# Expert tiles in four pieces, the last four tiles behind a branch

## The chip, the cores and the metric

The kernel runs on one core of one Trainium2 chip. The metric is the device time of one execution in microseconds (us). Engines are named as in the profile: PE (matmuls), PEld (its weight loads), DVE, ACT, POOL, and SP, which issues most DMAs.

## What is computed

A network of four blocks over 4096 tokens of 256 features: differential attention, a two-layer local attention with feed-forward, a diffusion block and a mixture of experts. Only the last one is touched. For each token a gate chooses two of eight experts; each expert is a two-layer network with a layer norm between:

```python
gates = jax.nn.softmax(xf @ gate_w, axis=-1)
topw, topi = jax.lax.top_k(gates, K)                 # K = 2 of E = 8
topw = topw / jnp.sum(topw, axis=-1, keepdims=True)
combine = jnp.sum(topw[:, :, None] * jax.nn.one_hot(topi, E, dtype=xf.dtype), axis=1)
h = jnp.einsum('td,edh->teh', xf, w1) + b1           # 256 -> 512
h = _ln(h, ln1_g, ln1_b)
h = jax.nn.gelu(h, approximate=False)
y = jnp.einsum('teh,ehd->ted', h, w2) + b2           # 512 -> 256
out = jnp.einsum('ted,te->td', y, combine)
out = _ln(out + xf, ln_g, ln_b)
```

## The kernel before

Routing. As each of eight sequences of 512 tokens leaves the diffusion block, `gate` ranks the experts and scatters each token's row twice into a DRAM table `xrows`, sorted by expert, with the token's number in an extra column. Each expert has room for all 4096 tokens. After the last sequence `table` (L1320) counts the rows of each expert, rounds up to tiles of 128 rows (`ntiles`), and sums them up (`end`); its last entry is the number of tiles that hold rows. From that it makes `table_`: for each of `TILES` = 2 x 4096 / 128 + 8 = 72 tiles the row where it starts and the offsets of its expert's weights. 72 is the most that any routing can need. Tiles past the last one with rows read rows that were filled in advance and write to rows that nobody reads.

Tiles. `experts` (L1355) walks over all 72 tiles, with all experts' weights in SBUF. `value` reads one entry of the table into a register of one engine. For tile n:

- `load` (L1377): SP loads 128 rows (`ex`, six buffers), up to four tiles ahead.
- `hidden` (L1383): DVE makes `eto`, the rows to which the results go (six buffers); PE transposes the rows (`ext`), ACT copies them (`exT`); PE multiplies by w1 (`ph`, two PSUM buffers); DVE adds the bias (`eh`), takes the statistics (`st`, `mv`); POOL makes the reciprocal deviation (`rs`, L172 and L173); DVE normalizes `eh` in place (L194).
- `outer` (L1400): PE transposes `eh` (`eht`), ACT takes the Gelu with the norm's scale and bias in four instructions (`ehT`), PE multiplies by w2 (`py`), DVE adds the bias (`ey`), POOL scatters the 128 rows to the DRAM table `yrows` at `eto` (L1413). `ext` and `eht` share three PSUM buffers.

The loop at L1466 does `hidden(n)` and then `outer(n - 3)`, so three tiles are on their way at once. `between()` puts small work between tiles: the diagonal matrices of combine weights `edw` for four sequences.

The order of instructions on each engine is made when the program is built, by a scheduler: it takes the program order as priority and moves a later instruction ahead where an earlier one is not ready by its model of the times. Within one engine the order is then fixed, and each instruction waits for those that it needs.

Finish. When all scatters have landed, `finish` (L1417) takes for each sequence the normalized input (`xfb`) and the two results of each token (`egot`) from DRAM, adds them with their weights on PE (`pz`), norms twice and adds the residual. Two of the `xfb` loads do not depend on the tiles.

One branch is there already: at L955 every engine loads a flag into a register, and L956 chooses between two variants of the diffusion block. The given inputs take the first, so that after it the code of the other is jumped over.

Of the kernel before, what the change touches and what calls it, by code (L numbers as in the profile page):

```python
# [16 lines left out]
P = 128  # L17
# [16 lines left out]
NE = 8  # L34
EH = 2 * D
EC = EH // P
CAP = NB * S
TILES = 2 * CAP // P + NE
ROWS = NE * CAP + NE * P
HOLD = 1000  # L40

# [79 lines left out]
class Net:  # L121
# [77 lines left out]
    def turned(self, ps, src, dst, scale=None, bias=None):  # L199

        nc = self.nc
        for c in range(src.shape[2] // P):
            pt = ps.tile([P, S], F32, name="pt", tag="ps")
            for t in range(NT):
                nc.tensor.transpose(pt[:, t * P:(t + 1) * P], src[:, t, c * P:(c + 1) * P], self.ident)
            if scale is None:
                self.copy(dst[:, c, :], pt)
            else:
                nc.scalar.activation(dst[:, c, :], pt, AF.Identity, bias=bias[:, c:c + 1], scale=scale[:, c:c + 1])
# [1014 lines left out]
    def load_routes(self, ctx):  # L1224

        w = ctx.enter_context(self.tc.tile_pool(name="routes", bufs=1))
        self.gatew = w.tile([P, DC, NE], F32, name="gate", tag="gate")
        self.nc.sync.dma_start(self.gatew, self.a["L1_ffn_gate_w"].rearrange("(c p) f -> p c f", p=P))
        self.routes = w
        self.slots = [w.tile([P, 2 * NT], mybir.dt.int32, name=f"slots{b}", tag=f"slots{b}") for b in range(NB)]  # L1230
        self.vals = [w.tile([P, 2, 2, NT], F32, name=f"val{b}", tag=f"val{b}") for b in range(NB)]
        self.runs = [w.tile([P, NT + 1, NE], F32, name=f"run{b}", tag=f"run{b}") for b in range(NB)]
        self.table_ = w.tile([P, 4, TILES], mybir.dt.int32, name="table", tag="table")

    def row_of(self, c, n):
        return self.const[:, c:c + n]
# [83 lines left out]
    def table(self, run, wk, small, ps):  # L1320

        nc, row = self.nc, self.row_of
        tie = row(C_TIE, NE * NE).rearrange("p (e f) -> p e f", f=NE)
        cap, tiles = CAP, TILES
        pc = ps.tile([P, NE], F32, name="pcount", tag="ps")
        self.mm(pc, [(row(C_ONE, P), run[:, NT, :])])
        n = small.tile([P, NE], F32, name="count", tag="count", bufs=1)
        nc.vector.tensor_copy(n, pc)
        thr = row(C_STEP, cap // P)
        over = small.tile([P, NE, cap // P], F32, name="over", tag="eover", bufs=1)  # L1330
        nc.vector.tensor_tensor(over, n.unsqueeze(2).to_broadcast([P, NE, cap // P]),
                                thr.unsqueeze(1).to_broadcast([P, NE, cap // P]), ALU.is_gt)
        nt = small.tile([P, NE], F32, name="ntiles", tag="ntiles", bufs=1)
        nc.vector.tensor_reduce(nt, over, AX.X, ALU.add)
        m = small.tile([P, NE, NE], F32, name="upto", tag="upto", bufs=1)
        nc.vector.tensor_mul(m, tie, nt.unsqueeze(1).to_broadcast([P, NE, NE]))
        end = small.tile([P, NE], F32, name="end", tag="end", bufs=1)
        nc.vector.tensor_reduce(end, m, AX.X, ALU.add)
        nc.vector.tensor_add(end, end, nt)
        ge = wk.tile([P, 2, tiles, NE], F32, name="past", tag="th")  # L1340
        tile_i = row(C_TILE, tiles)
        nc.vector.tensor_tensor(ge[:, 0], tile_i.unsqueeze(2).to_broadcast([P, tiles, NE]),
                                end.unsqueeze(1).to_broadcast([P, tiles, NE]), ALU.is_ge)
        nc.vector.tensor_mul(ge[:, 1], ge[:, 0], nt.unsqueeze(1).to_broadcast([P, tiles, NE]))
        es = small.tile([P, 2, tiles], F32, name="estart", tag="estart", bufs=1)
        nc.vector.tensor_reduce(es, ge, AX.X, ALU.add)
        f = small.tile([P, 4, tiles], F32, name="offsets", tag="offsets", bufs=1)
        nc.vector.tensor_sub(f[:, 0], tile_i, es[:, 1])
        nc.vector.tensor_scalar(es[:, 1], es[:, 0], float(cap), None, ALU.mult)
        nc.vector.scalar_tensor_tensor(f[:, 0], f[:, 0], float(P), es[:, 1], ALU.mult, ALU.add)  # L1350
        for i, by in enumerate((DC * EH, EH + D, 2 * EC)):
            nc.vector.tensor_scalar(f[:, 1 + i], es[:, 0], float(NE - 1), float(by), ALU.min, ALU.mult)
        nc.vector.tensor_copy(self.table_, f)

    def experts(self, nb, rest):  # L1355

# [4 lines left out]
        with ExitStack() as ctx:  # L1361
# [4 lines left out]
            nc, tc, g = self.nc, self.tc, self.ew  # L1366
# [6 lines left out]
            def value(i, k, engine, top):  # L1373
                return nc.values_load(self.table_[0:1, k, i:i + 1], engines=[engine], min_val=0, max_val=top,
                                      skip_runtime_bounds_check_because="the table's expert and row are bounded as they are made")

            def load(i):  # L1377
                x = wk.tile([P, D + 1], F32, name="ex", tag="ex", bufs=6)
                r = value(i, 0, mybir.EngineType.SP, ROWS - P)
                nc.sync.dma_start(x, self.rows[bass.ds(r, P), :])  # L1380
                return x

            def hidden(i, x):  # L1383
                to = small.tile([P, 1], mybir.dt.int32, name="eto", tag="eto", bufs=6)
                nc.vector.tensor_tensor(to, x[:, D:D + 1], self.const[:, C_DUMP + i:C_DUMP + i + 1], ALU.min)
                pt = pst.tile([P, DC, P], F32, name="ext", tag="pst")
                for c in range(DC):
                    nc.tensor.transpose(pt[:, c, :], x[:, self.tok(c)], self.ident)
                xT = wk.tile([P, DC, P], F32, name="exT", tag="exT")
                nc.scalar.copy(xT, pt)  # L1390
                e = value(i, 1, mybir.EngineType.PE, (NE - 1) * DC * EH)
                eb = value(i, 2, mybir.EngineType.DVE, (NE - 1) * (EH + D))
                ph = psh.tile([P, EH], F32, name="ph", tag="psh")
                self.mm(ph, [(xT[:, c, :], w1[:, bass.ds(e + c * EH, EH)]) for c in range(DC)])
                h = wk.tile([P, EH], F32, name="eh", tag="eh", bufs=4)
                nc.vector.tensor_add(h, ph, bias[:, bass.ds(eb, EH)])
                self.norm(small, [h], [h])
                return h, e, eb, to

            def outer(i, h, e, eb, to):  # L1400
                pt = pst.tile([P, EC, P], F32, name="eht", tag="pst")
                for c in range(EC):
                    nc.tensor.transpose(pt[:, c, :], h[:, self.tok(c)], self.ident)  # L1403
                en = value(i, 3, mybir.EngineType.Activation, (NE - 1) * 2 * EC)
                hT = wk.tile([P, EC, P], F32, name="ehT", tag="ehT")
                for c in range(EC):
                    nc.scalar.activation(hT[:, c, :], pt[:, c, :], AF.Gelu, bias=scales[:, bass.ds(en + EC + c, 1)],  # L1407
                                         scale=scales[:, bass.ds(en + c, 1)])
                py = psy.tile([P, D], F32, name="py", tag="psy")
                self.mm(py, [(hT[:, c, :], w2[:, bass.ds(e + c * D, D)]) for c in range(EC)])  # L1410
                y = wk.tile([P, D], F32, name="ey", tag="ey", bufs=4)
                nc.vector.tensor_add(y, py, bias[:, bass.ds(eb + EH, D)])
                i = nc.gpsimd.indirect_dma_start(self.got[:, :], bass.IndirectOffsetOnAxis(ap=to, axis=0), y, None)  # L1413
                tc.declare_no_dep(i.ins, group="store", reason="results have rows of their own")
                tc.add_to_no_dep_group("store", i.ins)
# [46 lines left out]
            between = Between()  # L1462
            for b in range(min(4, nb)):
                between.add(weights(b))
            loaded, made = {}, {}
            for n in range(TILES + 3):  # L1466
                for j in range(n, min(n + 4, TILES)):
                    if j not in loaded:
                        loaded[j] = load(j)
                if n < TILES:  # L1470
                    made[n] = hidden(n, loaded.pop(n))
                if n >= 3:
                    outer(n - 3, *made.pop(n - 3))
                between()
            between.end()
            tiles.close()
            psf = ctx.enter_context(tc.tile_pool(name="e_psf", bufs=6, space=PSUM))
            self.joint()
# [79 lines left out]
```

## Time and profile before

| what | us |
|---|---|
| median of three timed runs (lowest, highest) | 3854.63 (3848.53, 3860.05) |
| the profiled execution's own time | 3837.43 |
| its span, first to last instruction | 3835.7 |
| first and last expert transpose `ext` start | 3374.9, 3719.7 |
| first and last scatter of results start | 3401.88, 3740.41 |
| first `egot` load issued | 3742.8 |

The granted clock of PE was 0.953 on average over the span. The profile has, for each instruction, its start and length, and for each idle time of an engine what ended it. A line number can be that of a helper: `mm` (L213) issues most matmuls, so they are told apart by the tile's name. Lengths of matmuls overlap, since PE is pipelined.

### The profile page before, as it was taken

To read this page: it belongs to the slowest core of one execution; us is meant where nothing else is said; L and a number is where in the kernel's file an instruction comes from. 1 tells how busy PE (TensorE), PEld (TensorE's weight loads), DVE (VectorE), ACT (ScalarE), POOL (GpSimd) and SP (SyncE) were. 2 spreads that over 40 slices of the span, in tenths; PEclk is the share of its full clock that TensorE was granted. 3 is DMA by queue.
4 is the path that set the end of the run, shared out by engine and by line. 5 is a ranking of instruction groups with operands and counts; after the bars stand their busy time and mean duration, and the time that the engine had idled before them with its cause. 6 is when DMAs were issued, how large, how long until landed. Compare 5 with 4: busy or idle time off the path is not lost. (4 is left out here: it accounts for less than half of the span.)

```text
span 3835.7 us, 53567 instructions
## 1 busy us (share of the span) xinstructions
PE 3484.9 (91%) x20034; PEld 1894.1 (49%) x20034; DVE 2201.1 (57%) x4364; ACT 1855.1 (48%) x3719; POOL 1583.6 (41%) x1432
## 2 busy tenths in 40 slices
PE   8999999999987999999999999997988889679985
PEld 3344444444434566665665555564444444446554
DVE  6777777677646666665555666663244443344445
ACT  3555555555543444444444444443655555223334
POOL 3666766676654433333333343321012211153334
PEclk8999999999979999999999999998999999789997
DMA  9300000000001000000010000000000000421115
GB/s 350 119 1 7 6 7 1 7 7 1 6 6 34 3 4 4 4 4 25 4 34 9 9 9 9 9 20 23 1 23 23 23 17 17 147 68 55 53 43 167
DMA packets 95138, 130.29 MB, mean 34 GB/s; under 512 B 24702, under 2 KB 73242, under 8 KB 94874
## 3 DMA queue, kind: packets, MB, share of 16 engines
q1 hardware_dynamic: 88346, 108.94, 8.8%
q0 software_dynamic: 6528, 17.87, 1.3%
q8 instruction: 162, 2.65, 0.3%
q14 instruction: 102, 0.84, 0.1%
HBM read 57.40 MB, written 65.18 MB: 32 GB/s over the span
## 5 line engine op out<-in xcount | busy, mean ns | idle before, releaser
L372 ACT ACTIVATE e<-sa 128x1024 f32<-128x1024 f32 (+3 forms) x512 | 359.4, 702 | 303.7 <-PE sa L365 299.3
L393 POOL TENSOR_TENSOR e<-e,e 128x1536 f32<-128x1536 f32 (+2 forms) x192 | 451.7, 2353 | 91.4 <-PE po L388 81.4
L365 PE MATMUL sa<-qT,kT 32*128 32x512 f32 (+3 forms) x2048 | 431.9, 498 | 9.2 <-ACT e L372 8.8
L369 DVE TENSOR_REDUCE spread<-sc 128x2 f32<-128x256 f32 (+3 forms) x512 | 422.2, 825 | 15.3
L355 PE MATMUL sc<-kT,qT 32*128 32x128 f32 (+3 forms) x2048 | 421.6, 493 | 7.9 <-DVE spread L369 4.5
L656 ACT ACTIVATE lp<-lp,lnm 128x256 f32<-128x256 f32 (+1 forms) x512 | 240.1, 470 | 260.4 <-DVE lnm L648 156.0
L660 POOL TENSOR_TENSOR lp<-lp,lrs 128x1024 f32<-128x1024 f32 x64 | 121.1, 1893 | 529.0 <-DVE lrs L657 508.9
L368 DVE TENSOR_TENSOR sc<-sc,const 128x256 f32<-128x256 f32 x512 | 218.6, 427 | 173.7 <-PE sa L365 140.7
L1088 ACT ACTIVATE te<-tsa 128x1024 f32<-128x1024 f32 x256 | 248.9, 1023 | 135.8 <-PE tsa L1084 88.7
L355 PEld LDWEIGHTS sc<-kT,qT 32*128 32x128 f32 x2048 | 160.7, 189 | 284.9 <-DVE spread L369 113.1
L213 PE MATMUL lpa<-ghT,lw 128*128 128x512 f32 x640 | 284.8, 600 | 12.1 <-ACT ghT L569 12.1
L213 PE MATMUL lqk<-qkv,lhT 128*128 128x512 f32 x512 | 247.7, 622 | 2.3 <-DVE qk L607 1.6
L608 POOL TENSOR_TENSOR qk<-qk,over 128x1024 f32<-128x1024 f32 x64 | 151.4, 2366 | 207.8 <-DVE qk L607 207.8
L375 POOL TENSOR_SCALAR_AFFINE_SELECT e<-e 128x512 f32<-128x512 f32 x256 | 160.5, 640 | 177.0 <-ACT e L372 176.6
L1407 ACT ACTIVATE ehT<-eht,enorm 128x128 f32<-128x128 f32 x288 | 108.3, 457 | 208.6 <-PE eht L1403 207.7
L213 PEld LDWEIGHTS lpa<-ghT,lw 128*128 128x128 f32 x640 | 119.3, 190 | 163.3 <-issue 136.3
L388 PE MATMUL po<-e,v 128*32 128x512 f32 (+3 forms) x2048 | 188.3, 451 | 4.0 <-POOL e L375 3.6
L365 PEld LDWEIGHTS sa<-qT,kT 32*128 32x128 f32 x2048 | 160.9, 190 | 56.4 <-ACT e L372 29.7
L645 DVE TENSOR_TENSOR lp<-lsc,const 128x768 f32<-128x768 f32 (+1 forms) x128 | 138.6, 1083 | 86.5 <-PE lsc L642 85.9
L642 PE MATMUL lsc<-lkT,lqT 64*128 64x256 f32 (+1 forms) x1024 | 156.9, 386 | 28.1 <-DVE qk L607 28.0
L1084 PE MATMUL tsa<-tqT,tkT 32*128 32x512 f32 x1024 | 170.2, 673 | 5.9 <-DVE tqT L1039 3.3
L213 PE MATMUL py<-ew,ehT 128*128 x576 | 145.3, 397 | 23.5 <-ACT ehT L1407 23.5
(294 smaller groups left out, 6811.7 us busy)
## 6 DMA issues: line engine op xcount, KB each, us to landing
xrows<-zero SPq DMA_DIRECT2D x66, 514.0 KB
ex<-xrows SPq DMA_DIRECT2D x72, 128.5 KB
ew<-in_L_ffn_w_dram SPq DMA_DIRECT2D x16, 512.0 KB
egot<-yrows SPq DMA_DIRECT2D x16, 512.0 KB
x<-in_L_attn_X_dram SPq DMA_DIRECT2D x8, 512.0 KB
saved<-x SPq DMA_DIRECT2D x8, 512.0 KB
lx<-saved SPq DMA_DIRECT2D x8, 512.0 KB
xf<-xf SPq DMA_DIRECT2D x8, 512.0 KB
```

What stands on the lines that cost most here:

```text
L213: self.nc.tensor.matmul(out, lhsT=l, rhs=r, start=i == 0, stop=i == len(pairs) - 1)
L355: nc.tensor.matmul(sc[:, i, :w], lhsT=qT[g, self.tok(t)], rhs=kT[g, :w], start=True, stop=True)
L365: nc.tensor.matmul(sa[:, i, :S - k * P], lhsT=kT[g, self.tok(k)], rhs=qT[g, k * P:], start=True, stop=True)
L368: nc.vector.tensor_add(sc[:, :, w - P:w], sc[:, :, w - P:w], own)
L369: nc.vector.tensor_reduce(self.spread[n % 2][:, t, g0:g0 + 2, 0 if n % 2 else 16], sc[:, :, :w], AX.X, ALU.max, negate=True)
L372: nc.scalar.activation(x[:, h0:h0 + 2, :], sa[:, :, :S - k * P], AF.Exp, scale=0.25)
L375: nc.gpsimd.affine_select(x[:, :, :P], x[:, :, :P], [[0, 4], [1, P]], ALU.is_ge, 0.0, base=0, channel_multiplier=-1)
L388: nc.tensor.matmul(pos[n][group(g), k * P:], lhsT=seqs[b][1][:, k, 4 * r + g, :], rhs=x[:, g, :], start=k == 0, stop=k == 2)
L393: nc.gpsimd.tensor_add(y, y, es.pop((n, k)))
L656: nc.scalar.activation(x, x, AF.Exp, bias=nm[:, i, k:k + 1], accum_out=rs[:, i, k:k + 1])
L1084: m = nc.tensor.matmul(sa[i // 2][:, i % 2, :], lhsT=kT[q, self.tok(k)], rhs=qT[q, :], start=True, stop=True)
L1088: nc.scalar.activation(e[:, 2 * i:2 * i + 2, :], sa[i], AF.Exp)
```

## The change

The body of a tile is cut into four pieces instead of two: `front` (destination rows, transposes of the input and their copy), `hidden` (w1, bias, norm), `turned` (transposes of the hidden rows and Gelu) and `outer` (w2, bias, scatter). Within one iteration the order becomes front(n), turned(n - 3), hidden(n), outer(n - 3).

The loop becomes a function `through(first, end)` that fills and drains its own pipeline. It is called for tiles 0 to 67, and, after the work of `between` has ended, for tiles 68 to 71 within `tc.If(filled > SOME)`. `filled` is the number of tiles with rows, copied from `end` to an integer tile of its own by `table`; all five engines load it into a register.

```diff
@@ -36,6 +36,7 @@
 TILES = 2 * CAP // P + NE
+SOME = TILES - NE // 2
@@ -1231,6 +1232,7 @@
         self.table_ = w.tile([P, 4, TILES], mybir.dt.int32, name="table", tag="table")
+        self.filled = w.tile([P, 1], mybir.dt.int32, name="filled", tag="filled")
@@ -1351,6 +1353,7 @@
         nc.vector.tensor_copy(self.table_, f)
+        nc.vector.tensor_copy(self.filled, end[:, NE - 1:NE])
@@ -1380,7 +1383,7 @@
-            def hidden(i, x):
+            def front(i, x):
                 to = small.tile([P, 1], mybir.dt.int32, name="eto", tag="eto", bufs=6)
...
                 nc.scalar.copy(xT, pt)
+                return xT, to
+
+            def hidden(i, xT, to):
                 e = value(i, 1, mybir.EngineType.PE, (NE - 1) * DC * EH)
...
-            def outer(i, h, e, eb, to):
+            def turned(i, h, e, eb, to):
                 pt = pst.tile([P, EC, P], F32, name="eht", tag="pst")
...
+                return hT, e, eb, to
+
+            def outer(i, hT, e, eb, to):
                 py = psy.tile([P, D], F32, name="py", tag="psy")
@@ -1462,17 +1471,29 @@
-            loaded, made = {}, {}
-            for n in range(TILES + 3):
-                for j in range(n, min(n + 4, TILES)):
-                    if j not in loaded:
-                        loaded[j] = load(j)
-                if n < TILES:
-                    made[n] = hidden(n, loaded.pop(n))
-                if n >= 3:
-                    outer(n - 3, *made.pop(n - 3))
-                between()
+            def through(first, end):
+
+                loaded, made = {}, {}
+                for n in range(first, end + 3):
+                    for j in range(n, min(n + 4, end)):
+                        if j not in loaded:
+                            loaded[j] = load(j)
+                    if n < end:
+                        x = front(n, loaded.pop(n))
+                    if n >= first + 3:
+                        h = turned(n - 3, *made.pop(n - 3))
+                    if n < end:
+                        made[n] = hidden(n, *x)
+                    if n >= first + 3:
+                        outer(n - 3, *h)
+                    between()
+
+            through(0, SOME)
             between.end()
+            filled = nc.values_load(self.filled[0:1, :], min_val=0, max_val=TILES,
+                                    skip_runtime_bounds_check_because="it is bounded as it is made")
+            with tc.If(filled > SOME):
+                through(SOME, TILES)
             tiles.close()
```

## The prediction

> **What bounds the kernel now.** I read the engine totals first, then the busy time by stretch, then the waits and two pieces of the timeline in the stage that the diff touches. Over the whole span PE is busy 91%, but the change lives only in the expert stage, from the first expert transpose at 3374.9 us to the last scatter at 3740.4 us.
>
> ```profile
> PE 3484.9 (91%) x20034; PEld 1894.1 (49%) x20034; DVE 2201.1 (57%) x4364; ACT 1855.1 (48%) x3719; POOL 1583.6 (41%) x1432
> ```
>
> The stretches (columns: width, then busy us and count of PE, PEld, DVE, ACT, POOL, then clock, DMA share, GB/s) show PE at 46 of 50 us with full clock in mid-stage, and after 3745 a different stage, whose DMA share is 0.83:
>
> ```profile
> 3500.00:3550.00 50.00, 45.98 (x191) 30.74 (x190) 24.15 (x60) 18.50 (x53) 18.10 (x30) 1.00 0.18 55
> 3745.00:3790.00 45.00, 38.11 (x155) 31.22 (x156) 23.56 (x93) 28.25 (x82) 16.38 (x7) 0.92 0.83 266
> ```
>
> PE is not alone at the limit. The waits of 3400 to 3740 us (total, times, longest):
>
> ```profile
> DVE eto L1385 <- DMA yrows<-ey,eto: 88.6, 57, 3.1
> DVE eh L194 <- POOL rs L173: 73.6, 69, 2.2
> PE py L213 <- ACT ehT L1407: 23.5, 59, 0.4
> ```
>
> In a steady tile PE does ph, eht, ext, then stands 0.40 us until the first Gelu is done, then py. DVE meanwhile stands 1.5 us at eto, because eto has six buffers, each is read by a scatter, and the sixth-last scatter has not landed. One late tile in the timeline (start, length):
>
> ```profile
> 3691.55 0.42 DVE L1412 TENSOR_TENSOR ey<-py,ebias 128x256 f32<-128x256 f32 x1
> 3692.25 1.06 POOL L1413 DMA_INDIRECT yrows<-ey,eto  x1 [1.20 <-DVE ey L1412]
> 3694.76 0.16 DVE L1385 TENSOR_TENSOR eto<-ex,const 128x1 int32<-128x1 f32 x1 [1.47 <-DMA yrows<-ey,eto]
> 3694.84 0.17 DVE L186 BATCH_NORM_AGGREGATE mv<-st 128x2 f32<-128x6 f32 x1
> 3695.98 0.55 DVE L194 TENSOR_SCALAR eh<-eh,mv,rs 128x512 f32<-128x512 f32 x1 [0.96 <-POOL rs L173]
> 3696.44 0.42 DVE L1412 TENSOR_TENSOR ey<-py,ebias 128x256 f32<-128x256 f32 x1
> 3697.15 1.06 POOL L1413 DMA_INDIRECT yrows<-ey,eto  x1 [1.21 <-DVE ey L1412]
> ```
>
> That is a closed loop: scatter to eto 2.51, eto to mv 0.08, mv to norm 1.14 (through POOL), norm to ey 0.46, ey to next scatter 0.71: 4.90 us a tile. PE alone runs 4.77 us (ACT's exT copies follow at 4.77). PE goes first until its buffers are used up, then waits for DVE: from 3651 us on, all engines step at 4.90. The 72 scatters run from 3401.88 to 3740.41 us, 338.5 us for 71 intervals, 4.77 on average.
>
> **The change part by part.** *Four tiles fewer.* The routing of the given inputs, evaluated from the reference, counts 674, 1594, 611, 701, 883, 1836, 1015 and 878 rows for the eight experts: 6+13+5+6+7+15+8+7 = 67 tiles of 128. The nearest expert to a further tile has 9 rows to spare, and two would have to cross, so 67 is not above 68 and the branch is skipped. Each dropped tile takes from PE 18 matmuls and 18 weight loads, from DVE six instructions, from ACT five, from POOL two and a scatter, from SP a register load and a 128.5 KB load. Fill and drain stay, so at the old pace it is worth 4 x 4.77 = 19.1 us.
>
> *Four pieces.* Program order within an iteration was ext, ph, eht, py; it becomes ext, eht, ph, py. `turned` (four transposes on PE, a register load and four Gelus on ACT) passes `hidden` (ph, a PE and a DVE register load, DVE's add, statistics and norm, POOL's two rs). No DMA moves: the SP load stays ahead of front, the POOL scatter last. On ACT the Gelus still come after the same tile's exT copy. The Gelus now have ph's 1.7 us to run in, so the 0.40 us stall of PE should go. The instruction scheduler may still hoist, so I take evidence from the stage's start, where PE happens to run ext, eht, ext, ph, py:
>
> ```profile
> 3407.17 0.55 DVE L194 TENSOR_SCALAR eh<-eh,mv,rs 128x512 f32<-128x512 f32 x1 [2.05 <-POOL rs L173]
> 3407.66 0.69 DVE L1396 TENSOR_TENSOR eh<-ph,ebias 128x512 f32<-128x512 f32 x1
> 3408.27 0.15 DVE L1385 TENSOR_TENSOR eto<-ex,const 128x1 int32<-128x1 f32 x1
> 3409.01 0.42 DVE L1412 TENSOR_TENSOR ey<-py,ebias 128x256 f32<-128x256 f32 x1
> 3409.60 1.98 PE L213 MATMUL ph<-ew,exT 128*128 x4
> 3409.72 1.07 POOL L1413 DMA_INDIRECT yrows<-ey,eto  x1 [2.59 <-DVE mv L186]
> 3411.73 0.55 DVE L194 TENSOR_SCALAR eh<-eh,mv,rs 128x512 f32<-128x512 f32 x1 [2.21 <-POOL rs L173]
> ```
>
> With ph directly followed by py, ey falls ahead of the norm, and eto no longer waits for a scatter. What is late next is POOL: rs queues behind the scatter that is now ahead of it, and DVE's norm, with the next add behind it, waits for rs. Norm to norm is 4.56 here, 4.69 in the next tile, 4.52 at 3424.20 to 3428.72: mean 4.59. PE itself is faster (three tiles of exT copies from 3409.70 to 3422.36: 4.22 each; the next three 4.30), so POOL and DVE set the pace. 68 tiles have 67 intervals: 67 x 4.59 = 307.5 us against 338.5, a gain of 31.0 us, of which 19 are the dropped tiles.
>
> *The branch.* The trace has one such branch (L955 and L956):
>
> ```profile
> L955 DVEq TENSOR_LOAD <-iflag x1: 548/548/548, 2660.4 to 2660.4; - x1
> L956 PEldq COMPARE_BRANCH  x2: 95/1981/3867, 2654.8 to 3297.4; - x2
> L956 SPq COMPARE_BRANCH  x2: 38/48/57, 2670.1 to 3278.6; - x2
> ```
>
> Each engine passes it at its own time; no common barrier is seen. Entering costs a 0.47 to 0.55 us register load and 0.04 to 0.1 us; leaving, a jump over the other variant's long code, cost PE 3.87 us. The Trainium skill, "Runtime: NRT & Kernel Launch", section on instruction fetch mechanics, says that a taken branch whose target is outside the current two-page window stalls until the page is fetched, and calls run-time control flow expensive for it. That speaks against this change, which jumps always. Its jump is short (144 PE instructions of matmul and weight load, a few dozen elsewhere), so the near value is L956's small one, 0.6 us with the load; by the rule's worst case 3.87 + 0.55 = 4.4 us. Either is covered: PE has 7 us between its last py (ends 3739.7) and the first pz that needs data (3746.81), DVE and ACT over 10 us, POOL until 3758, and SP issued its last ex at 3695. If the join makes SP wait for the others, the 4.4 us come on top.
>
> *What can't cross the branch.* Two xfb loads (512 KB each) ran at 3423.9 us, within the tiles; they now come after it. If SP runs through early, they cost nothing: they land before the last scatter. If not, they join the egot loads: 1.05 MB at 266 GB/s is 3.9 us. The eight early pz matmuls (1.99 us) and ACT's table load (1.28 us) lie under the wait for egot. One more copy on DVE for `filled` (about 0.17 us, like L1303's) lies under POOL's scatters that end at 3371. A gain is excluded, since nothing here is taken away. For branch and loads together: 0 to 8.3 us; I take 2, near the low end, as the nearest rows show no barrier.
>
> Sum: -31.0 + 2 = -29 us. The profiled execution took 3837.43 us (span 3835.7), so 3808; the median of the timed runs lies 17.2 us higher, at 3854.63, and I predict against that: 3826 us.
>
> **The rivals.** *PE alone is the bound.* If POOL's rs is queued ahead of the scatter, the POOL loop opens and PE's 4.30 holds: 67 x 4.30 = 288.1, -50.4 + 2: 3806 us. For it: PE kept 4.22 to 4.30 for several tiles. Against: only while it used up its lead over DVE.
>
> *The scatter loop stays.* If norm stays ahead of ey behind eto, the loop is 4.90 whatever PE does: 67 x 4.90 = 328.3, -10.2 + 2 = -8: 3846 us, the dropped tiles half given back. For it: it is the order of most tiles now. If the pace stays at the mean 4.77 instead, 319.6 us, -17: 3838.
>
> *Slower.* eto, issued first in an iteration, could be queued just ahead of the next add (eh), since eh now comes a longer time after ey. Then the add (0.72) and the statistics (about 0.7) fall inside the scatter loop: 4.90 + 1.4 = 6.3 us a tile, 67 x 6.3 = 422, +84 + 2: 3940 us. It decides above (338.5 - 2)/67 = 5.02 us a tile. Against: in the start's like-ordered tiles eto stands after the add.
>
> *The branch is taken after all*, a count above 68: four tiles at the new pace (18 us) and a second fill and drain (about 14 us, the drain seen from 3726.8 to 3740.4) eat the gain: about 3858. The counts speak against.
>
> **How the numbers follow.** Forecast 0.45; PE bound 0.20; pace unchanged at 4.77 0.08; scatter loop 0.17; slower 0.07; branch taken 0.03. About 0.3%, 11.6 us, can be told from no change: the scatter loop mostly falls within it. Faster 0.77, within 0.14, slower 0.09. The range reaches from PE bound with nothing added to the scatter loop with some branch cost: 3800 to 3850.
>
> **What would show it.** Right: 68 scatters; no DVE wait of eto for yrows, or a small one; PE py without the 0.40 us wait; POOL rs waiting on the scatter; scatter intervals near 4.6; the compare-branch of the new If under 0.2 us and egot's first issue about 2.4 us after the last scatter, as now. Wrong: intervals of 4.9 with the eto wait still there, or over 5 with eh behind eto; a gap of over 3 us between last scatter and egot; xfb loads after that gap.

## The result: slower by 1.4%, in two places where the forecast had put no cost

The changed kernel takes 3899.56 us at the median (six runs, 3890.55 to 3905.89), the kernel before 3851.58 us beside it (six runs, 3831.29 to 3860.05). The ratio is 1.014 with a 95% interval of 1.0115 to 1.0165. The profiled execution took 3890.55 us, at a mean granted clock of 0.955 (0.953 before). Its span is 3888.8 us against 3835.7, so there are 53.1 us to explain. Cut at three instants that both traces have:

| stretch | before, us | after, us | difference |
|---|---|---|---|
| start to the first expert transpose | 3374.9 | 3367.0 | -7.9 |
| first transpose to the last scatter | 365.5 | 400.8 | +35.3 |
| last scatter to the end | 95.3 | 121.0 | +25.7 |

The first row lies in stages that the edit does not touch. Its 8 us are already there at 1134 us, part of them before 50 us, and they are the kind of amount by which executions differ. The other two rows are the effect.

The branch is skipped: the trace has 68 scatters. Busy time by engine hardly tells what happened, but one entry does. ACT does less tile work and is busy 42.2 us longer (1855.1 before):

```profile
PE 3448.3 (89%) x19962; PEld 1880.0 (48%) x19962; DVE 2196.4 (56%) x4341; ACT 1897.3 (49%) x3731; POOL 1592.7 (41%) x1420
```

**The tiles.** After a first interval of 2.58 us, the next eight between scatters are 4.46, 4.77, 4.53, 4.54, 6.26, 4.53, 4.53 and 4.68 us. That is the forecast pace, and DVE runs in the forecast order, norm (L195), the next add, eto, statistics, ey. The eto here begins 3.12 us after the latest scatter and does not wait for it (timeline of after; start, length):

```profile
3410.23 1.06 POOL L1422 DMA_INDIRECT yrows<-ey,eto  x1 [2.56 <-DVE mv L187]
3412.24 0.55 DVE L195 TENSOR_SCALAR eh<-eh,mv,rs 128x512 f32<-128x512 f32 x1 [2.21 <-POOL rs L174]
3412.74 0.69 DVE L1402 TENSOR_TENSOR eh<-ph,ebias 128x512 f32<-128x512 f32 x1
3413.35 0.15 DVE L1388 TENSOR_TENSOR eto<-ex,const 128x1 int32<-128x1 f32 x1
3413.47 0.69 DVE L185 BATCH_NORM_STATS2 st<-eh 128x6 f32<-128x512 f32 x1
3414.08 0.41 DVE L1421 TENSOR_TENSOR ey<-py,ebias 128x256 f32<-128x256 f32 x1
3416.78 0.55 DVE L195 TENSOR_SCALAR eh<-eh,mv,rs 128x512 f32<-128x512 f32 x1 [2.21 <-POOL rs L174]
```

Then two intervals of 5.23 and 5.79 us follow, and from 3445.79 us on the stage steps at 6.04, but for two intervals at one place (8.56 and 5.79) and the last five (3.10 down to 1.27), where the pipeline drains. One such tile:

```profile
3482.07 1.32 POOL L1422 DMA_INDIRECT yrows<-ey,eto  x1 [0.19 <-issue]
3484.85 0.16 DVE L1388 TENSOR_TENSOR eto<-ex,const 128x1 int32<-128x1 f32 x1 [2.39 <-DMA yrows<-ey,eto]
3485.34 0.69 DVE L1402 TENSOR_TENSOR eh<-ph,ebias 128x512 f32<-128x512 f32 x1 [0.33 <-issue]
3486.07 0.69 DVE L185 BATCH_NORM_STATS2 st<-eh 128x6 f32<-128x512 f32 x1
...
3486.80 0.18 DVE L187 BATCH_NORM_AGGREGATE mv<-st 128x2 f32<-128x6 f32 x1
3486.92 0.42 DVE L1421 TENSOR_TENSOR ey<-py,ebias 128x256 f32<-128x256 f32 x1
3487.07 0.19 POOL L173 TENSOR_SCALAR rs<-mv 128x1 f32<-128x1 f32 x1 [3.68 <-DVE mv L187]
3487.34 0.57 POOL L174 TENSOR_TENSOR rs<-rs,mhalf 128x1 f32<-128x1 f32 x1
3488.11 1.32 POOL L1422 DMA_INDIRECT yrows<-ey,eto  x1 [0.19 <-issue]
```

Read it as a circle (`ey` and the norm hang on it, but are not part of it): scatter to eto 2.78, eto to the add 0.49, add to statistics 0.73, statistics to mv 0.73, mv to rs 0.27, and rs to the next scatter 1.04: 6.04 us. The eto of a coming tile waits for a scatter that has just been issued, because they share one of the six eto buffers. The add, which needs nothing of it, stands behind it in DVE's order, and so does the register load for its bias. ey is done early here, but its scatter stands behind the two rs on POOL, which come from that add. Over all 68 tiles eto waited for a scatter as follows (total, times; 88.6 and 57 before):

```profile
  DMA yrows<-ey,eto: 128.7, 55
```

The 67 intervals take 373.9 us, 5.58 on average.

**The end.** The way through the branch costs nothing that the end can see: egot's first issue comes 2.41 us after the last scatter, 2.42 before.

```profile
3767.78 0.96 POOL L1422 DMA_INDIRECT yrows<-ey,eto  x1 [1.45 <-DVEq L1495]
3770.19 2.04 SPq L1431 DMA_DIRECT2D egot<-yrows  x4
```

The row names DVE's branch as the releaser of the last scatter, but the scatter starts 0.70 us after its ey (3767.08), and 0.71 is the usual distance in the prediction's loop, so it was not held. The branch's own instructions (line views of after; min, median, max in ns, first and last start):

```profile
L1493 ACTq TENSOR_LOAD <-filled x1: 375/375/375, 3354.0 to 3354.0; - x1
L1493 DVEq TENSOR_LOAD <-filled x1: 314/314/314, 3767.1 to 3767.1; - x1
L1495 SPq COMPARE_BRANCH  x1: 50/50/50, 3717.7 to 3717.7; - x1
L1495 PEldq COMPARE_BRANCH  x1: 359/359/359, 3766.5 to 3766.5; - x1
L1495 POOLq COMPARE_BRANCH  x1: 55/55/55, 3768.4 to 3768.4; - x1
```

But see where ACT's register load stands: at 3354.0 us, ahead of the tiles, where the scheduler hoisted it. The load of the activation table that holds Ln and Exp together, which `joint()` asks for after the branch, stands right behind it, at 3354.4. The first Gelu then loads its own table at 3376.45, and what the finish finds is that one. So each Ln and each Exp of the finish loads a table by itself:

```profile
L967 ACT ACT_TABLE_LOAD  x3: 1283/1283/1283, 6.0 to 3354.4; - x3
L170 ACT ACT_TABLE_LOAD  x16: 1283/1283/1283, 3782.6 to 3876.6; - x16
L171 ACT ACT_TABLE_LOAD  x16: 1283/1283/1283, 3784.5 to 3878.2; - x16
```

Before, the third joint load came at 3738.4 us, after the last Gelu, and L170 and L171 loaded nothing in the finish. Now there are 32 loads of 1.283 us, 41 us on ACT, and the finish is 25.7 us longer. The timeline shows how DVE waits for one:

```profile
3784.47 1.28 ACT L171 ACT_TABLE_LOAD   x1
3785.77 0.20 ACT L171 ACTIVATE rs<-rs 128x4 f32<-128x4 f32 x1
3786.01 0.16 DVE L1452 SCALAR_TENSOR_TENSOR nm<-mv,rs 128x4 f32<-128x4 f32 x1 [1.59 <-ACT rs L171]
```

In mid-finish ACT is the busiest engine, with 18.82 of 20 us. The first line is of after, from 52 us behind its last scatter, the second of the kernel before, from 38 us behind its own (columns: width, busy us and count of PE, PEld, DVE, ACT, POOL, clock, DMA share, GB/s):

```profile
3820.00:3840.00 20.00, 9.29 (x43) 7.85 (x41) 8.37 (x37) 18.82 (x30) 8.87 (x4) 0.84 0.53 177
```

```profile
3778.00:3798.00 20.00, 14.42 (x50) 11.80 (x51) 11.73 (x38) 11.70 (x28) 9.72 (x5) 0.83 0.70 235
```

### The profile page after: what moved, and what is told of

The parts are those of the page before. It is cut to its first block, busy times and chain, and to the rows that moved or that the text cites. A ratio compares the mean times of both kernels' runs of the same rounds, so it can differ in the third digit from the quotient of the medians.

```text
span 3888.8 us, 53384 instructions
## 1 busy us (share of the span) xinstructions
PE 3448.3 (89%) x19962; PEld 1880.0 (48%) x19962; DVE 2196.4 (56%) x4341; ACT 1897.3 (49%) x3731; POOL 1592.7 (41%) x1420
## 5 line engine op out<-in xcount | busy, mean ns | idle before, releaser
L657 ACT ACTIVATE lp<-lp,lnm 128x256 f32<-128x256 f32 (+1 forms) x512 | 240.1, 470 | 262.4 <-DVE lnm L649 157.6
L214 PE MATMUL ph<-ew,exT 128*128 x272 | 137.8, 631 | 87.4 <-ACT ehT L1413 77.5
L665 POOL TENSOR_TENSOR lp<-lp,lrs 128x256 f32<-128x256 f32 (+1 forms) x128 | 103.2, 828 | 140.9 <-DVE lrs L658 140.9
```

What stands on the lines that cost most here:

```text
L214: self.nc.tensor.matmul(out, lhsT=l, rhs=r, start=i == 0, stop=i == len(pairs) - 1)
L657: nc.scalar.activation(x, x, AF.Exp, bias=nm[:, i, k:k + 1], accum_out=rs[:, i, k:k + 1])
```

## The experiments

The theory was: eto, queued ahead of the add and waiting for a scatter, costs the tiles; the table load, placed before the tiles, costs the finish; the two add up, and the skipped branch itself is worth about four tiles. The rivals: the order of four pieces costs by another way (PE, POOL), the branch costs by itself, or a single further buffer of eto would do. Ratios to the kernel before are compared, since the groups of runs were on different chips and the kernel before itself reads 3811 to 3852 us there. Intervals are those between scatters; "finish" is the last scatter to the end.

| kernel | us | before beside it | ratio (95%) | intervals: sum, mean | finish, us |
|---|---|---|---|---|---|
| before | | | 1 | 338.5 / 71 = 4.77 | 95.3 |
| after | 3899.56 | 3851.58 | 1.014 (1.0115-1.0165) | 373.9 / 67 = 5.58 | 121.0 |
| order_only | 3899.07 | 3837.94 | 1.0147 (1.01-1.0194) | 394.6 / 71 = 5.56 | 96.0 |
| branch_only | 3848.75 | 3837.94 | 1.0021 (1.0008-1.0035) | 323.9 / 67 = 4.83 | 120.5 |
| after_tables | 3872.50 | 3837.94 | 1.0081 (1.0053-1.0108) | 373.7 / 67 = 5.58 | 96.8 |
| after_eto | 3808.64 | 3837.94 | 0.9902 (0.987-0.9934) | 290.1 / 67 = 4.33 | 120.4 |
| after_both | 3761.22 | 3811.25 | 0.9865 (0.9831-0.9899) | 290.1 / 67 = 4.33 | 96.2 |
| both7 | 3843.07 | 3811.25 | 1.0087 (1.0053-1.0121) | 371.6 / 67 = 5.55 | 94.2 |
| order_eto | 3780.49 | 3811.25 | 0.9907 (0.987-0.9943) | 307.9 / 71 = 4.34 | 96.4 |
| before_eto | 3796.84 | 3811.25 | 0.9963 (0.9952-0.9973) | 324.4 / 71 = 4.57 | 94.5 |
| pinned | 3798.15 | 3842.97 | 0.9875 (0.9859-0.9892) | 290.1 / 67 = 4.33 | 96.4 |
| both8 | 3871.38 | 3842.97 | 1.0080 (1.0063-1.0098) | 369.5 / 67 = 5.51 | 97.5 |
| both10 | 3872.48 | 3842.97 | 1.0070 (1.005-1.009) | 380.1 / 67 = 5.67 | 97.0 |
| branch_tables | 3821.21 | 3842.97 | 0.9952 (0.994-0.9965) | 321.1 / 67 = 4.79 | 95.0 |

### The change taken apart: order_only and branch_only

order_only has the four pieces, over all 72 tiles and without the branch:

```diff
-            through(0, SOME)
+            through(0, TILES)
...
-            filled = nc.values_load(self.filled[0:1, :], min_val=0, max_val=TILES,
-                                    skip_runtime_bounds_check_because="it is bounded as it is made")
-            with tc.If(filled > SOME):
-                through(SOME, TILES)
```

> The four pieces alone: all 72 tiles in one pipeline, no branch. Theory (two causes: eto stands ahead of the next tile's add on DVE and waits for a scatter that ends only after it, a loop of 6.04 us a tile; and the norms of the finish load an activation table before each Ln and Exp, because of the branch): slower than before by 75 us, some ten scatter intervals near 4.5 and then 6.04 each; finish stage (last scatter to end) 95 us as before, no table loads at L170 or L171. Rival (the slow tiles come from the branch, which the scheduler treats as a unit): pace 4.3 to 4.8, at most 10 us from before.

branch_only has the branch with the old order inside an iteration:

```diff
                     if n < end:
                         x = front(n, loaded.pop(n))
+                        made[n] = hidden(n, *x)
                     if n >= first + 3:
                         h = turned(n - 3, *made.pop(n - 3))
-                    if n < end:
-                        made[n] = hidden(n, *x)
-                    if n >= first + 3:
                         outer(n - 3, *h)
```

> The old order ext, ph, eht, py in one iteration, with 68 tiles and the last four in the branch. Theory: scatter intervals 4.77 on average, so 4 x 4.77 = 19 us less in the tiles; 32 table loads in the finish, 26 us more there: together +7 us against before. Rival (skipping the branch itself is dear): a gap between last scatter and first egot of more than 3 us, and more than +10 us. Rival (the branch is cheap and the order of the four pieces brings the table loads): -19 us and no table loads.

The order alone gives the slow tiles: steady steps of 6.04 us, intervals 56.1 us longer in sum than before's (394.6 - 338.5), a measured 1.47% of 3837.94, which is also 56, and a finish of 96.0 us without table loads. Some 75 us had been expected: ten intervals near 4.5 and the rest at 6.04. What that left out is the drain, whose last five intervals take 11.5 us, not 30.2. The branch alone gives the slow finish with 32 table loads, at tiles that stay in before's loop of 4.90. Its eto waits are before's too (line of the groups, window 3380 to 3700 us; the figures after the bar are busy us, mean ns, and the idle time before it with its parts):

```profile
L1388 DVE TENSOR_TENSOR eto<-ex,const 128x1 int32<-128x1 f32 x65 | 10.3, 159 | 98.2 <-DMA yrows<-ey,eto 85.2 <-DMA ex<-xrows 13.0
```

Intervals -14.7 and finish +25.2 make +10.5 us by the profiles; 0.21% is 8. So each half of the change carries one of the two costs.

### Each cost taken away: after_tables, after_eto, after_both

after_tables puts a one-element ACT copy, into a PSUM buffer that the finish is about to use, ahead of `joint()`. The pool of that buffer opens after the tiles' pools have been closed, so the copy and the table load behind it stay there:

```diff
             psf = ctx.enter_context(tc.tile_pool(name="e_psf", bufs=6, space=PSUM))
+            nc.scalar.copy(psf.tile([P, 2, D], F32, name="pz", tag="psf")[:, 0, 0:1], self.const[:, 0:1])
             self.joint()
```

> The changed kernel with the preload of the joint Ln and Exp table made to come after the branch: a one-element copy into a PSUM buffer of the finish stands ahead of it, since the preload follows ACT's previous instruction. Theory: the 32 table loads vanish, the finish falls from 121 to about 95 us, tiles unchanged at 6.04: 24 to 27 us less than the changed kernel, about +22 against before. Rival (the finish is long because of the branch's join or of later loads from DRAM): finish still near 120 us and less than 5 us gained.

The finish falls to 96.8 us, the L170 and L171 loads are gone, and the joint load stands at 3769.7 us, behind the tiles. The tiles are unchanged at 373.7 us. So the table load's place is 24.1 us of the 25.7 us of the second cost.

```profile
L967 ACT ACT_TABLE_LOAD  x3: 1283/1283/1283, 6.2 to 3769.7; - x3
```

ACT's register load is no longer hoisted here either: it starts at 3766.6 us. The two move together: both are early in after (3354.0 and 3354.4), branch_only (3368.6 and 3369.0) and after_eto, both late in after_tables, branch_tables (3715.8 and 3719.6) and pinned. Which of them draws the other is not shown.

after_eto gives eto twelve buffers and changes nothing else:

```diff
-                to = small.tile([P, 1], mybir.dt.int32, name="eto", tag="eto", bufs=6)
+                to = small.tile([P, 1], mybir.dt.int32, name="eto", tag="eto", bufs=12)
```

> The changed kernel with twelve buffers for eto instead of six, nothing else. Theory: the scatter whose landing eto waits for is then six tiles older, the loop opens, and PE sets the pace at 4.3 us a tile: 67 x 4.3 = 288 us instead of 374, so about 85 us less than the changed kernel, -37 to -25 against before with the table loads still there. Rival (POOL's order of rs and scatter holds DVE): 4.55 a tile, -8 against before. Rival (the three PSUM buffers shared by ext and eht, or psh, hold the tiles): still near 6 us and no gain.

The intervals fall from 373.9 to 290.1 us, 4.33 each, with the slow finish kept. Against after that is 83.8 us on an index tile of 512 bytes. after_both makes both edits:

> The changed kernel with both cures: twelve eto buffers, and the table preload held behind the branch. Theory: the gains add up, tiles at 4.33 us as with twelve buffers alone, finish 96 us as with the preload alone: about 24 us less than twelve buffers alone, 3784 against 3838 before, -53 us. Rival (the finish waits for DRAM loads once the tiles are faster): less than 15 us better than twelve buffers alone.

It is 1.35% faster than before, and this is where the change's promise was. The steady step is 4.45 us, and the list of waits from 3400 to 3640 us has none of PE, which is busy 49.11 of every 50 us in mid-stage, so PE sets this pace; the short intervals of the drain bring the mean to 4.33. eto still stands in front of the add, as in after, but waits only for its input, and the add would have had to wait for PE in any case (timeline of after_both):

```profile
3562.56 0.16 DVE L1388 TENSOR_TENSOR eto<-ex,const 128x1 int32<-128x1 f32 x1 [0.82 <-DMA ex<-xrows]
3563.06 0.69 DVE L1402 TENSOR_TENSOR eh<-ph,ebias 128x512 f32<-128x512 f32 x1 [0.34 <-PE ph L214]
...
3565.66 0.55 DVE L195 TENSOR_SCALAR eh<-eh,mv,rs 128x512 f32<-128x512 f32 x1 [0.60 <-POOL rs L174]
...
3567.03 0.16 DVE L1388 TENSOR_TENSOR eto<-ex,const 128x1 int32<-128x1 f32 x1 [0.82 <-DMA ex<-xrows]
```

### How many buffers, or which place: both7, both8, both10, pinned

If one spare buffer were enough, seven would do. both7 is after_both with `bufs=7`:

```diff
-                to = small.tile([P, 1], mybir.dt.int32, name="eto", tag="eto", bufs=12)
+                to = small.tile([P, 1], mybir.dt.int32, name="eto", tag="eto", bufs=7)
```

> As the version with both cures, with seven eto buffers instead of twelve. Theory: one more buffer gives the scatter a whole tile more to land (2.8 us needed, over 4 us given), so the same time as with twelve, within 5 us. Rival (landing has a long tail, or the scheduler moves eto one tile earlier, up to the next scatter): a DVE wait of eto for yrows over 0.5 us a tile and over 15 us slower than twelve.

That expectation fell. The steps are 6.04 us again, eto waits 126.3 us at 54 tiles, and the wait has not moved by a hundredth:

```profile
3562.83 0.16 DVE L1388 TENSOR_TENSOR eto<-ex,const 128x1 int32<-128x1 f32 x1 [2.39 <-DMA yrows<-ey,eto]
3563.32 0.69 DVE L1402 TENSOR_TENSOR eh<-ph,ebias 128x512 f32<-128x512 f32 x1 [0.33 <-issue]
```

The order of instructions on DVE says why. Count how many more eto than ey stand in it up to and with a steady tile's eto; call it the lead. It is six with six buffers (before and after), seven with seven. The scheduler places eto as early as a buffer allows, so that the wait is always for the latest scatter. The next two runs ask how far that goes, both8 with `bufs=8` and both10 with `bufs=10` in the same line:

> Both cures with eight eto buffers. Seven looped as six did: the scheduler moved eto one tile further ahead and let it wait for the same newest scatter. Theory: how far ahead eto can run is bounded by the six ex buffers; a buffer more of eto is used up until that bound is met. With eight the row that eto(i + 8) needs can be loaded once tile i + 2 is transposed, which is before scatter i, so the loop stays: 6.04 us a tile, +0.9% against before. Rival (a fixed landing time of 2.8 us is met with one or two tiles more): 4.4 us a tile.

> Both cures with ten eto buffers. Theory: eto(i + 10) needs rows that are loaded only after tile i + 4 is transposed, later than scatter i; then ex, not eto, bounds how far ahead it runs: 4.33 us a tile as with twelve, -1.3% against before, and waits for ex in place of waits for yrows. Rival (the wait follows every buffer that is added): still 6.04 us a tile.

both8 did as expected (lead 8, steps of 6.04, wait of 123.7 us at 52 tiles). both10 was expected to be free and is not: its lead is 10, and eto waits 130.8 us at 49 tiles, with steps of 6.04 and some near 8.

```profile
3561.42 0.16 DVE L1388 TENSOR_TENSOR eto<-ex,const 128x1 int32<-128x1 f32 x1 [2.39 <-DMA yrows<-ey,eto]
```

With twelve buffers the lead is 10 as well (11 at one tile). The scatter whose buffer eto then needs is two older than the latest, and eto waits for its rows instead (ex, 49.3 us at 49 tiles in after_both). That suggests that the six buffers of ex set the lead of 10; no run gave ex more buffers, and eleven buffers of eto were not tried.

The other cure leaves six buffers and takes the lead away. In pinned, eto is made behind the add and is kept there (the table load is pinned as in after_both):

```diff
-                to = small.tile([P, 1], mybir.dt.int32, name="eto", tag="eto", bufs=6)
-                nc.vector.tensor_tensor(to, x[:, D:D + 1], self.const[:, C_DUMP + i:C_DUMP + i + 1], ALU.min)
...
-                return xT, to
+                return xT, x
...
-            def hidden(i, xT, to):
+            def hidden(i, xT, x):
...
                 nc.vector.tensor_add(h, ph, bias[:, bass.ds(eb, EH)])
+                to = small.tile([P, 1], mybir.dt.int32, name="eto", tag="eto", bufs=6)
+                tc.keep_in_program_order(nc.vector.tensor_tensor(
+                    to, x[:, D:D + 1], self.const[:, C_DUMP + i:C_DUMP + i + 1], ALU.min))
```

> Six eto buffers as in the change, table preload held behind the branch; eto is made in hidden(n), straight behind the same tile's add, and held there, so that the scheduler can't take it ahead. Theory (what costs is that eto runs ahead of its tile up to the newest scatter, not the number of buffers): its buffer was last read by a scatter issued three tiles earlier, no wait for yrows, 4.33 to 4.45 us a tile, within 8 us of the version with twelve buffers and preload (about -1.3% against before). Rival (six buffers are too few wherever eto stands): waits for yrows stay and the time is over 1% above that version.

It ties with after_both (0.9875 against 0.9865, with overlapping intervals) at the same 4.33 us. The lead is 4, no eto waits for a scatter, and DVE's add now waits for PE:

```profile
3560.14 0.69 DVE L1400 TENSOR_TENSOR eh<-ph,ebias 128x512 f32<-128x512 f32 x1 [1.30 <-PE ph L214]
3560.75 0.15 DVE L1402 TENSOR_TENSOR eto<-ex,const 128x1 int32<-128x1 f32 x1
...
3564.58 0.69 DVE L1400 TENSOR_TENSOR eh<-ph,ebias 128x512 f32<-128x512 f32 x1 [1.30 <-PE ph L214]
```

Here too the steady step is 4.45 us without a wait of PE, although the scatter still stands behind the two rs on POOL and takes 1.32 us: that place alone does not cost. What matters is that eto runs ahead up to the newest scatter; of the buffer numbers tried, only the one above the lead of 10 helps.

### What each part is worth without the costs: order_eto, before_eto, branch_tables

order_eto is order_only with twelve eto buffers, before_eto the kernel before with them. branch_tables is branch_only with the copy ahead of `joint()`, at six buffers. Their edits are those shown above.

> Four pieces, twelve eto buffers, all 72 tiles, no branch. Theory: 4.33 to 4.4 us a tile, 71 intervals, finish 96 us without table loads: the branch is worth its four tiles, so 17 us more than both cures, -35 against before. Rival (the branch costs several us of join and code jump): less than 12 us more than both cures.

> The kernel before with twelve eto buffers, nothing else. Theory: PE's own chain in the old order (0.40 us for the first Gelu) gives 4.77 us a tile, so only the late tiles at 4.90 and the odd longer ones gain: -3 to -8 us. Rival (the scatter loop held all tiles of the old order, and the order of pieces is worth nothing without it): 4.3 to 4.5 us a tile, -20 to -33 us.

> The old order of pieces, six eto buffers, 68 tiles and four in the branch, table preload held behind the branch. Theory: 67 intervals of 4.77 to 4.84 and a finish of 96 us: the four tiles less the branch's own cost, -14 to -19 us against before, 24 us less than without the preload. Rival (the branch's join costs what the tiles save): within 5 us of before.

The branch is worth what four tiles are. branch_tables gains 0.48% of 3842.97, 18 us, and its intervals are 17.4 us shorter than before's; after_both's are 17.8 us shorter than order_eto's. The order of four pieces is worth 307.9 - 324.4 = -16.5 us in intervals once eto is free in both. before_eto gains 14 us where 3 to 8 were expected. Its steady steps are the 4.77 us that PE's own work sets, as expected. What was underrated are the steps of before: not only the late tiles but nearly all from the twelfth interval on step at 4.90 us or more. Between the first eleven intervals and the last five, 55 intervals take 262.4 us in place of 276.3, which is nearly all of the gain.

## Why the prediction was wrong

**The dropped tiles and the branch: right, but for its neighbours.** The branch is skipped, each engine passes it at its own time (SP at 3717.7, the others from 3765.0 to 3768.4 us), and egot comes about 2.4 us after the last scatter: all as forecast. Four tiles were put at 19.1 us and measured 17 to 18. The worst cases of 4.4 us for the jump and 3.9 us for late xfb loads did not come. The xfb loads crossed the branch, the first at 3413.4 us, among the first tiles: "they now come after it" was wrong.

**The four pieces: the forecast order held for nine tiles.** The forecast was 4.59 us a tile, and seven of the eight intervals after the first are 4.46 to 4.77 us. The step that failed is "I take evidence from the stage's start", and with it "eto no longer waits for a scatter": an order that was built for some tiles at the start was taken for all 68. In after it holds for nine eto (the eighth to the sixteenth). From then on eto stands in front of the add, and what the runs show in place of the forecast is 128.7 us of waits for scatters at 55 tiles, steps of 6.04 us and a mean of 5.58.

The six buffers were in full use in the evidence already. Its eto at 3408.27 is the eighth, and needs the buffer of the latest scatter (3405.26 us, in the timeline of before), not of an older one, as "the sixth-last scatter" suggests. It did not wait only because norm and add stood before it, so that it came 3.01 us after that scatter, where 2.5 are enough. The prediction's own row, 88.6 us at 57 tiles, said that eto mostly comes too early. Whoever moves work behind such a wait has to ask, for every instruction behind it, what hangs on it.

The rival "Slower" had the mechanism, the place and nearly the price, 6.3 us for the measured 6.04, and the measured mean is past its point of decision, 5.02. It got 0.07 because of one piece of evidence that did not bear on most of the stage. Its 3940 us was too high by some 48 us in the intervals: 17 because a step is 6.04 us, the rest because the first ten intervals and the five of the drain are shorter.

Two smaller readings were off. 4.22 and 4.30 us for PE come from the starts of Gelus in three uneven tiles each (3409.70 and 3422.36 are no exT copies); PE's steady step in the new order is 4.45. And 67 x 4.59 leaves out the drain: its five last intervals take 11.5 us in after, where five at 4.59 are 23.0, while the 338.5 us of before include the drain.

**"What can't cross the branch": the term that was mis-sized.** The table load was costed at nothing, because 1.28 us "lie under the wait for egot". That holds where it stands behind the last Gelu. The prediction asked what the branch would hold back, and the change did the reverse. The table load was hoisted ahead of the tiles together with ACT's new register load for the branch, and the first Gelu put its own table in its place. Its price is then not one load but 32, and 24.1 us in the finish (121.0 against 96.8 in after_tables); bounds of 0 to 8.3 us for "branch and loads together" had no room for it.

**The sum** was 31.0 gained, 2 lost. It came to 35.3 lost in the tiles (their fill included), 25.7 lost in the finish, and 7.9 gained in earlier stages, which the edit does not explain. Without the two costs the gain is there and larger. after_both is 1.35% faster, some 51 us, at 4.33 us a tile; the rival "PE alone is the bound" (4.30, 50.4 gained) would then have had the right bound, and its sum comes out because the short intervals of the drain make up for a steady step of 4.45.

**What stays open:** why the scheduler places eto behind the add in the nine tiles at the start and before it from then on. The trace shows the order that was built, not its reasons, and no run tried to change them. That the table load and ACT's register load were hoisted together is read from their starts; which one draws the other is open, and the runs show only that a copy that can't be hoisted brings both back behind the tiles.

## What to carry to other kernels

When an instruction waits for a buffer that a DMA reads, look at how far the built order runs it ahead of that DMA, not only at the number of buffers: give it more buffers than the lead that its input allows (here twelve against 10), or pin it behind the work that must not wait. An order seen in the first tiles of a loop is evidence for those tiles alone; look at the middle of the loop as well. After a branch is put in, look at what was set up before it and is needed behind it, such as an activation table: a load that is free in one place costs once per use in another.

## What the runs showed of the hardware that had not been expected

A scatter's issue on POOL takes 1.06 us in 61 of the 72 tiles of before, where POOL had been idle for 1.2 us or more, and 1.32 us in 52 of the 68 of after, where it stands directly behind the two rs. Where eto waits for a scatter, it mostly started 2.52 us after that scatter's issue began before the change, and 2.78 after: 1.46 us after the end of the issue in both. DVE's register load for the next bias takes 0.30 us (median) in order with its arithmetic, and shows as a 0.33 us wait of "issue" behind eto. A short jump over the four tiles' code costs 50 to 69 ns on most engines and 359 ns on PE, against the 3.87 us of the long jump in the trace of before (3.53 in after's).
